# Laying the end of batch 0's latent attention beside the next stage of a hybrid two-layer kernel

## Chip, core and metric

The program runs on one core of one Trainium2 chip. The metric is the device time of one execution in microseconds (us). The time before is the median of three runs. One execution was also taken with the hardware profiler; it carries the trace that is quoted here.

## The reference, cut to what matters

Two batches of 1024 tokens with 128 channels pass through eight residual blocks. The first four are of interest:

```
x = x + latent_attention(layernorm(x))     # 16 heads, keys and values from a latent of 32, causal
x = x + spiking_ffn(layernorm(x))          # relu^2 layer, five steps of a spiking neuron: a count of spikes / 5
x = x + state_space(layernorm(x))          # convolution, per-token step sizes, a scan along the tokens
x = x + spiking_ffn(layernorm(x))
... linear attention, experts, attention over heads, experts
```

The latent attention is a softmax over earlier tokens: `softmax(mask(q k / 8)) v`, then the output projection and the residual add. Its softmax needs row maxima, exponentials, sums, the inverse of the sums and a product with it. The spiking layer reads every channel of a token after the attention has been added. The batches are independent of each other in all of these blocks.

## The kernel before

The first layer does not run block by block. While one batch is in one block, the other is in another, and the order in which the instructions stand on each engine is written out by hand: every step is a Python generator, and `weave(main, side, rate)`, `alternate(...)` and `among(...)` decide whose turn it is. Inside `tc.manual_schedule(engines=ALL)` the instructions go to the engines in just this order. Each engine works through its own queue in order, so an instruction that waits holds up all that stand behind it.

The order at the place of the change:

1. Row maxima of batch 0 (`row_maxima(0, ...)`), then its attention, `attend(0, ...)`. The attention works on two halves of 512 query tokens (`Half`), each over 4 groups of heads (`C = 4`). The end of the first half is drawn out between the steps of the second half. The end of the second half is run through alone after the last step (`for _ in end: yield`).
2. `Half.end()` is that end: ScalarE copies the sums (`rec`, L438), VectorE takes the reciprocal (L439), and then, for each of the four groups, TensorE spreads the inverse sums over the rows with a matmul by `pick` (L446) and VectorE multiplies `oU` by them (L454). Sixteen matmuls by `wvo` (L459) give the projected output in PSUM, and VectorE adds it to the tokens `x_res` (L469).
3. Constants of the state space (`StateConstants`) come next in the program.
4. The next stage is `weave(into_space(0, bank), maxima, 1.1)`. Its main stream is `into_space(0, ...)`: spiking layer of tokens 0 to 511, spiking layer of tokens 512 to 1023 beside the first tokens of the state space, then the rest of the projections and step sizes of the state space. Its side stream is `maxima = row_maxima(1, ...)`, the row maxima of batch 1: 48 units, each of four (or, where a block touches the diagonal, eight) matmuls (L265, L274) into two PSUM tiles, and two VectorE reductions (L283). After each step of the main stream `due` grows by 1.1 and as many units follow. After the 48 units the maxima are split into three bf16 terms (L288 to L297), turned by TensorE (L301) and copied to `nmT` (L302).
5. The loop of the state space of batch 0, `space[0].loop(...)`, in 32 iterations: SyncE loads two tiles of 512 KB (`s_a` and `s_h`, L751) from DRAM, ScalarE makes decays (L760), VectorE multiplies, scans and multiplies (L791, L792, L793). Woven into it as side stream is `attend(1, ...)`, the attention of batch 1, which needs `nmT` (L364).

What the loads of step 5 need: the step sizes of the first 128 channels, which VectorE finishes in `s_delta` (L713) and `s_dtx` (L715) and SyncE writes to DRAM (L714, L716); and the place of the buffers of stage 4 in SBUF, of which the last read is the matmul by `skip_wT` (L618).

PSUM has 8 banks. In step 4 two of them are the pool `bank`, which the main stream rotates through, and six are the three two-bank tiles of the maxima, `a_s`. In step 2 the tiles `a_st` of the attention are used.

The last steps of the main stream in step 4 come from `alternate(s.first_sizes(1), s.rest(1))`. On TensorE they are the products by `wb8T`, by `wc8T`, by `skip_wT`, by `wd2T` and again by `skip_wT` (all L618).

Of the kernel before, what the change touches and what calls it, by code (L numbers as in the profile page):

```python
# [9 lines left out]
F32 = mybir.dt.float32  # L10
# [9 lines left out]
P = 128  # L20
# [71 lines left out]
def weave(main, side, rate):  # L92

    due = 0.0
    for _ in main:
        due += rate
        while due >= 1.0:
            next(side, None)
            due -= 1.0


def alternate(*streams):

    streams = list(streams)
    while streams:
        for steps in list(streams):
            try:
                next(steps)
            except StopIteration:
                streams.remove(steps)  # L110
                continue
            yield
# [16 lines left out]
def drain(steps):  # L129
    for _ in steps:  # L130
        pass
# [20 lines left out]
class LatentAttention:  # L152
# [149 lines left out]
        nc.vector.tensor_copy(self.nmT[b], pt.rearrange("p a b -> p (a b)"))  # L302
        yield

    def attend(self, b, work, ps, ps_o, added=False, beside=iter(())):

        halves = [self.Half(self, b, half, work, ps, ps_o, added) for half in range(2)]  # L310
        units = [(h, c, kb) for h in halves for c in range(self.C) for kb in range(h.last + 1)]
        n = len(units)
        held, end = {}, iter(())

        for step in range(n + 3):
            if step < n:
                h, c, kb = units[step]
                held[step] = h.exponentials(c, kb)
            for back in (2, 3):
                if 0 <= step - back < n:  # L320
                    h, c, kb = units[step - back]
                    if back == 2:
                        h.weigh(c, kb, *held.pop(step - 2))
                    elif added and kb == h.last:
                        h.total_denominators(c)
                    if back == 2 + added and c == self.C - 1 and kb == h.last:
                        drain(end)
                        end = h.end()
            next(end, None)
            yield  # L330
        for _ in end:
            yield
            next(beside, None)
        yield from beside

    class Half:


        def __init__(self, latent, b, half, work, ps, ps_o, added):
            self.latent, self.b, self.half = latent, b, half  # L340
            self.work, self.ps, self.ps_o, self.added = work, ps, ps_o, added
            self.last = 4 * half + 3
            self.oTs, self.total = {}, {}

# [63 lines left out]
        def weigh(self, c, kb, pTs, off):  # L408
            latent, nc = self.latent, self.latent.g.nc
            last = kb == self.last  # L410
            if kb == 0:
                self.oTs[c] = self.ps_o.tile([P, 512], F32, name="a0_oT")
            for j in range(latent.J):
                nc.tensor.matmul(
                    self.oTs[c][32 * j : 32 * j + 32, off:],
                    latent.lat[self.b][:, kb, :],
                    pTs[j // 2][:, j % 2, off:],
                    start=(kb == 0),
                    stop=last,
                )  # L420
            if not self.added:
                self.denominators(c, pTs, off, c == 0 and kb == 0, c == latent.C - 1 and last)
            elif kb > 0:
                for k, pT in enumerate(pTs):
                    total = self.total[c, k][:, :, off:]
                    nc.vector.tensor_add(total, total, pT[:, :, off:])
            if last:
                if c == 0:
                    self.oU = self.work.tile([P, latent.C, 512], F32, name="a0_oU")
                nc.scalar.copy(self.oU[:, c, :], self.oTs.pop(c))  # L430

        def end(self):


            latent, g, nc, C = self.latent, self.latent.g, self.latent.g.nc, self.latent.C
            oU = self.oU
            rec = self.work.tile([P, 512], F32, name="a0_rec")
            nc.scalar.copy(rec, self.dT)  # L438
            nc.vector.reciprocal(rec, rec)  # L439
            yield  # L440
            if self.half == 0:
                for _ in range(2):
                    yield
            for c in range(C):
                rr = self.ps.tile([P, 2, 512], F32, name="a0_st")
                nc.tensor.matmul(rr[:, 0, :], latent.pick[:, c, :], rec, start=True, stop=True)  # L446
                if self.half == 0:
                    rs = self.work.tile([P, 512], F32, name="a0_rs", bufs=2)
                    nc.scalar.copy(rs, rr[:, 0, :])
                    nc.vector.tensor_mul(oU[:, c, :], oU[:, c, :], rs)  # L450
                    if c % 2:
                        yield
                else:
                    nc.vector.tensor_mul(oU[:, c, :], oU[:, c, :], rr[:, 0, :])  # L454
            yield
            pf = self.ps.tile([P, 2, 512], F32, name="a0_st")[:, 0, :].rearrange("p (a b) -> p a b", a=4)
            for i in range(4):
                for c in range(C):
                    nc.tensor.matmul(  # L459
                        pf[:, i, :], oU[:, c, bass.ts(i, P)], latent.wvo[:, c, :], start=(c == 0), stop=(c == C - 1)  # L460
                    )
            t = self.b * TPB + 4 * self.half
            xt = g.x[:, t : t + 4, :]
            if self.half == 0:
                add = self.work.tile([P, 4, D], F32, name="a0_rs", bufs=2)
                nc.scalar.copy(add, pf)
                nc.gpsimd.tensor_add(xt, xt, add)
            else:
                nc.vector.tensor_add(xt, xt, pf)  # L469
            yield  # L470
# [1032 lines left out]
def first_layer(g, w, open_experts, load_expert):  # L1503
# [3 lines left out]
    def pool(stack, name, bufs, **kw):  # L1507
        return stack.enter_context(tc.tile_pool(name=name, bufs=bufs, **kw))
# [5 lines left out]
    right = dict(side="right")  # L1514
    ends, latents, spaces = ExitStack(), ExitStack(), ExitStack()
    latent = LatentAttention(g, w, pool(latents, "a0_keep", 1, **right))
    own = pool(latents, "a0_batch1", 1, **right)
    with ExitStack() as es:
        latent.project([pool(es, "a0_batch0", 1), own])
        with tc.tile_pool(name="a0_seq", bufs=1) as seq, tc.tile_pool(name="a0_ps_a", bufs=2, space=PSUM) as ps:  # L1520
            drain(latent.row_maxima(0, seq, ps, 4))
        work = pool(es, "a0_work", 2)
        ps, ps_o = pool(es, "a0_ps_b", 3, space=PSUM), pool(es, "a0_ps_o", 1, space=PSUM)
        with tc.manual_schedule(engines=ALL):
            drain(latent.attend(0, work, ps, ps_o, added=True))

    bank = banks(spaces, "bank", 2)
    shared = StateConstants(g, w, pool(spaces, "s_one", 1))
# [43 lines left out]
    with tc.manual_schedule(engines=ALL):  # L1572
        with (
            tc.tile_pool(name="a0_seq", bufs=1, **right) as aseq,
            tc.tile_pool(name="a0_ps_a", bufs=3, space=PSUM, **right) as ps,
        ):
            maxima = latent.row_maxima(1, aseq, ps, 2)
            weave(into_space(0, bank), maxima, 1.1)
            drain(maxima)
        work = pool(latents, "a0_work", 1, **right)  # L1580
        ps, ps_o = pool(latents, "a0_ps_b", 2, space=PSUM, **right), pool(latents, "a0_ps_o", 1, space=PSUM, **right)

        spikes = spiking_steps(g, w, [2], Borrowed(work), lambda name: ps.tile([P, 2, 512], F32, name="a0_st")[:, 0, :])
        attend = latent.attend(1, work, ps, ps_o, beside=spikes)
        with tc.tile_pool(name="s_work", bufs=1, reuse_waits="tile") as work:
            side = among(space[0].late(), attend, 2)
            weave(space[0].loop(work, bank), side, 2.1)
        drain(side)
        latents.close()
        open_experts()  # L1590
        behind = batch0_behind()
        next(behind)
        with ExitStack() as es:
            weave(into_space(1, banks(es, "bank1", 3, **right), begun=True), behind, 0.85)
        with tc.tile_pool(name="s_work", bufs=1, reuse_waits="tile") as work:
            side = among(space[1].late(), behind, 2)
            weave(space[1].loop(work, bank), side, 2.1)
        spaces.close()
        with ends, ExitStack() as es:
            weave(out_of_space(1, banks(es, "bank", 3), abreast=True), side, 0.5)  # L1600
            drain(side)
# [115 lines left out]
```

## Time and profile before

| | us |
|---|---|
| median of three runs | 2140.3 (2138.62 to 2142.33) |
| the profiled execution, its own time | 2130.55 |
| span of the trace in it | 2128.5 |

| engine | busy us | share of the span |
|---|---|---|
| TensorE (PE) | 1844.5 | 87% |
| VectorE (DVE) | 1590.1 | 75% |
| ScalarE (ACT) | 1146.8 | 54% |
| GpSimd (POOL) | 923.6 | 43% |

Times in the profile count from the start of the span. The shares are means over the whole program; the change lies at 266 to 437 us, where the shares are others. A matmul on 32-bit operands shows as two passes, so four instructions are "x8" in a row. "PEclk" is the TensorE clock that was granted, as a share of full speed. "Idle before" is time in which the engine had nothing running ahead of the instruction, with the one that released it. "SPq" is SyncE's queue, which issues DMAs.

### The profile page before, as it was taken

What the parts mean: (1) busy time and instruction counts of PE and PEld (TensorE: products, weight loads), DVE (VectorE), ACT (ScalarE), POOL (GpSimd) and SP (SyncE); (2) the same over time, 40 slices, a digit from 0 to 9 for tenths busy, and PEclk for the clock granted to TensorE, in tenths of its full rate; (3) what the DMA queues carried; (4) which work ended last, traced back from release to release, by engine and by line L of the source; (5) the groups of instructions that cost most, each with busy time, mean ns of one, the idle gap of its engine ahead of it and who ended that gap; (6) DMA issues with size and microseconds to landing.
All of it is one profiled execution on the core that took longest, in us unless ns stands there. A gap on an engine that the chain in (4) does not pass through costs nothing. (4 is left out here: it accounts for less than half of the span.)

```text
span 2128.5 us, 29668 instructions
## 1 busy us (share of the span) xinstructions
PE 1844.5 (87%) x11616; PEld 1011.0 (47%) x11616; DVE 1590.1 (75%) x1846; ACT 1146.8 (54%) x1577; POOL 923.6 (43%) x510
## 2 busy tenths in 40 slices
PE   7679888979977757899678899999999999999999
PEld 4223243323334422334356565666565666566754
DVE  5976866898775679896432798999899999998222
ACT  1026612265643457683433677777777777777422
POOL 1013411055411210000110288989898888989400
PEclk9989978989997978999899999999999999999999
DMA  4000000097643077660000466666666666666000
GB/s 94 1 1 2 1 1 1 20 213 173 156 113 119 11 168 180 156 155 4 0 1 0 111 176 159 178 167 182 163 174 169 179 176 176 169 179 180 14 6 5
DMA packets 73771, 219.73 MB, mean 103 GB/s; under 512 B 9184, under 2 KB 19872, under 8 KB 73504
## 3 DMA queue, kind: packets, MB, share of 16 engines
q1 hardware_dynamic: 54736, 149.40, 23.8%
q0 software_dynamic: 18432, 67.12, 16.5%
q8 instruction: 91, 1.49, 0.3%
q10 hardware_dynamic: 464, 1.33, 0.3%
q14 instruction: 48, 0.39, 0.1%
HBM read 78.35 MB, written 5.24 MB: 39 GB/s over the span
## 5 line engine op out<-in xcount | busy, mean ns | idle before, releaser
L1345 POOL TENSOR_TENSOR h_e<-h_e,h_r 128x2048 f32<-128x2048 f32 x128 | 601.6, 4705 | 71.5 <-ACT h_r L1330 40.1
L1290 ACT ACTIVATE h_e<-h_e 128x1024 f32<-128x1024 f32 x256 | 256.6, 1049 | 165.5 <-DVE h_e L1287 164.8
L1281 DVE TENSOR_REDUCE h_m<-h_s 128x128 f32<-128x2048 f32 x128 | 293.2, 2290 | 52.1 <-PE h_s L1270 49.2
L1287 DVE TENSOR_TENSOR h_e<-h_s,h_m 128x2048 f32<-128x2048 f32 x128 | 293.2, 2290 | 9.1 <-DVE h_m L1281 0.5
L381 POOL TENSOR_SCALAR_AFFINE_SELECT a_pT<-a_pT 128x256 f32<-128x256 f32 x120 | 131.7, 1120 | 203.5 <-ACT a_pT L378 200.8
L283 DVE TENSOR_REDUCE a_nm<-a_s 128x2 f32<-128x1024 f32 (+7 forms) x144 | 168.1, 1217 | 40.4 <-PE a_s L274 26.2
L1270 PE MATMUL h_s<-h_qz,h_kT 32*128 32x512 f32 x1024 | 147.6, 645 | 40.2 <-DVE h_e L1287 38.8
L1111 PE MATMUL h_po<-e_h,Wd 128*128 128x256 f32 x640 | 172.2, 388 | 3.8 <-DVE e_h L1070 2.1
L378 ACT ACTIVATE a_pT<-a_st 128x1024 f32<-128x1024 f32 (+3 forms) x176 | 129.9, 791 | 64.9 <-PE a_st L364 63.4
L792 DVE TENSOR_TENSOR_SCAN s_h<-s_a,s_h 128x1024 f32<-128x1024 f32 x64 | 148.7, 2323 | 18.4 <-ACT s_a L760 14.4
L1298 POOL DMA_DIRECT2D h_e<-h_e x128 | 132.2, 1033 | 61.9 <-DMA h_e<-h_e 46.3
L1303 PE MATMUL h_pd<-ident,h_e 128*128 128x128 f32 x1024 | 138.4, 278 | 16.9 <-DMA h_e<-h_e 10.1
L1303 PEld LDWEIGHTS h_pd<-ident,h_e 128*128 128x128 f32 x1024 | 113.4, 141 | 79.7 <-DMA h_e<-h_e 34.2
L265 PE MATMUL a_s<-a_latT,a_qT 32*128 32x512 f32 (+3 forms) x768 | 115.8, 584 | 40.4 <-DVE a_nm L283 38.3
L1350 PE MATMUL h_po<-h_e,h_vz 128*32 128x256 f32 x2048 | 138.4, 388 | 0.8 <-POOL h_e L1345 0.6
L355 PE MATMUL a_st<-a_qT,a_latT 32*128 32x512 f32 (+3 forms) x768 | 119.2, 554 | 9.2 <-ACT a_pT L378 7.0
L958 ACT ACTIVATE e_sg<-e_pg 128x512 f32<-128x512 f32 x96 | 57.3, 597 | 129.5 <-PE e_pg L955 107.0
L1111 PEld LDWEIGHTS h_po<-e_h,Wd 128*128 128x128 f32 x640 | 111.9, 192 | 30.9 <-DVE e_h L1070 16.1
L963 DVE TENSOR_TENSOR e_h<-e_sg,e_pu 128x512 f32<-128x512 f32 x96 | 64.5, 684 | 82.3 <-PE e_pu L956 70.2
L956 PE MATMUL e_pu<-e_uT,Wu 128*128 128x512 f32 x192 | 102.0, 613 | 19.7 <-DVE e_h L963 19.7
L1084 PE MATMUL e_pgu<-e_uT,Wg 128*128 128x256 f32 x480 | 115.9, 382 | 0.0
L1084 PE MATMUL e_pgu<-e_uT,Wu 128*128 128x256 f32 x480 | 115.0, 380 | 0.5 <-ACT e_sg L1090 0.5
(303 smaller groups left out, 3203.9 us busy)
## 6 DMA issues: line engine op xcount, KB each, us to landing
h_e<-h_e SPq DMA_DIRECT2D x128, 512.0 KB, 3.4
h_e<-h_e POOLq DMA_DIRECT2D x128, 512.0 KB, 5.0
s_a<-s_steps SPq DMA_DIRECT2D x64, 512.0 KB, 5.1
s_h<-s_steps SPq DMA_DIRECT2D x64, 512.0 KB, 6.6
s_steps<-s_gate SPq DMA_DIRECT2D x8, 256.0 KB, 2.0
Wg<-in_Wg_dram SPq DMA_DIRECT2D x8, 256.0 KB, 5.9
Wu<-in_Wu_dram SPq DMA_DIRECT2D x8, 256.0 KB, 5.9
Wd<-in_Wd_dram SPq DMA_DIRECT2D x8, 256.0 KB, 6.0
```

What stands on the lines that cost most here:

```text
L283: nc.vector.tensor_reduce(nm[:, half, i, h : h + together], s[:, :, :n], AX.X, ALU.max, negate=True)
L792: nc.vector.tensor_tensor_scan(h, a, h, 0.0, ALU.mult, ALU.add)
L1084: self.g.nc.tensor.matmul(pgu[:, k, :], self.w[name][:, e, bass.ts(fc, P)], uT, start=True, stop=True)
L1111: nc.tensor.matmul(self.sums, self.w["Wd"][:, e, fc, :], h, start=False, stop=last, skip_group_check=True)
L1270: nc.tensor.matmul(s[:, j, :].rearrange("p (k q) -> p k q", k=K), kTs[b][quad, bass.ts(kb, P)], qzs[b][qb // 4][quad, :, bass.ts(qb % 4, P ...
L1281: nc.vector.tensor_reduce(m, heads.rearrange("p h q -> p q h"), AX.X, ALU.max)
L1287: nc.vector.tensor_sub(e, heads, m.unsqueeze(1).to_broadcast([P, H, P]))
L1290: nc.scalar.activation(eh, eh, AF.Exp, scale=scale)
L1298: nc.gpsimd.dma_start(out=e2, in_=e[:, 8:16, :], accum_op=ALU.add)
L1303: nc.tensor.matmul(pd[:, t, :], pair[:, t, k, :], g.ident, start=(t == 0 and k == 0), stop=(k == 7), is_transpose=True, skip_group_check=True,
L1345: nc.gpsimd.tensor_mul(e, e, r.unsqueeze(1).to_broadcast([P, H, P]))
L1350: nc.tensor.matmul(po[32 * j : 32 * j + 32, :], vz[:, kb * J + j, two].rearrange("p a d -> p (a d)"), a[:, 4 * j + 2 * two : 4 * j + 2 * t ...
```

## The change

`attend` takes a pool `late`. With it, the tiles `oU` and `rec` of the second half lie in that pool, which stays open through the next stage, and `attend` hands back the rest of the end instead of running through it. The copy of the sums and the reciprocal are still issued in `attend`. The rest of the end, from the first `pick` matmul on, becomes a stream of six steps: one for each group, one bare step, and one with the sixteen `wvo` matmuls and the add. This stream alternates with the steps of `into_space(0, ...)` in the main stream of step 4. Its PSUM tiles come from the two-bank pool `bank`.

```diff
-    def attend(self, b, work, ps, ps_o, added=False, beside=iter(())):
+    def attend(self, b, work, ps, ps_o, added=False, beside=iter(()), late=None):
         halves = [self.Half(self, b, half, work, ps, ps_o, added) for half in range(2)]
+        halves[1].keep = late or work
...
             next(end, None)
             yield
+        if late:
+            self.left_over = halves[1], end
+            return
         for _ in end:
...
+            self.bank = lambda: ps.tile([P, 2, 512], F32, name="a0_st")[:, 0, :]
...
-            rec = self.work.tile([P, 512], F32, name="a0_rec")
+            rec = self.keep.tile([P, 512], F32, name="a0_rec")
...
             for c in range(C):
-                rr = self.ps.tile([P, 2, 512], F32, name="a0_st")
-                nc.tensor.matmul(rr[:, 0, :], latent.pick[:, c, :], rec, start=True, stop=True)
+                rr = self.bank()
+                nc.tensor.matmul(rr, latent.pick[:, c, :], rec, start=True, stop=True)
...
                 else:
-                    nc.vector.tensor_mul(oU[:, c, :], oU[:, c, :], rr[:, 0, :])
+                    nc.vector.tensor_mul(oU[:, c, :], oU[:, c, :], rr)
+                    if self.keep is not self.work:
+                        yield
             yield
-            pf = self.ps.tile([P, 2, 512], F32, name="a0_st")[:, 0, :].rearrange("p (a b) -> p a b", a=4)
+            pf = self.bank().rearrange("p (a b) -> p a b", a=4)
...
+    late = ExitStack()
+    late_pool = pool(late, "a0_late", 1, **right)
...
-            drain(latent.attend(0, work, ps, ps_o, added=True))
+            drain(latent.attend(0, work, ps, ps_o, added=True, late=late_pool))
...
-            weave(into_space(0, bank), maxima, 1.1)
+            half, end = latent.left_over
+            half.bank = lambda: bank("a0_end")
+            weave(alternate(end, into_space(0, bank)), maxima, 1.1)
             drain(maxima)
+        late.close()
```

The instructions are the same in kind and number, save for their places in the queues of TensorE and VectorE; the queues of ScalarE, GpSimd and SyncE keep their order.

More of the change, by code (lines that the diff above doesn't have):

```diff
@@ L340, in __init__ @@
             self.latent, self.b, self.half = latent, b, half
-            self.work, self.ps, self.ps_o, self.added = work, ps, ps_o, added
+            self.work, self.ps, self.ps_o, self.added, self.keep = work, ps, ps_o, added, work
+            self.bank = lambda: ps.tile([P, 2, 512], F32, name="a0_st")[:, 0, :]
             self.last = 4 * half + 3
@@ L428, in weigh @@
                 if c == 0:
-                    self.oU = self.work.tile([P, latent.C, 512], F32, name="a0_oU")
+                    self.oU = self.keep.tile([P, latent.C, 512], F32, name="a0_oU")
                 nc.scalar.copy(self.oU[:, c, :], self.oTs.pop(c))
@@ L444, in end @@
             for c in range(C):
-                rr = self.ps.tile([P, 2, 512], F32, name="a0_st")
-                nc.tensor.matmul(rr[:, 0, :], latent.pick[:, c, :], rec, start=True, stop=True)
+                rr = self.bank()
+                nc.tensor.matmul(rr, latent.pick[:, c, :], rec, start=True, stop=True)
                 if self.half == 0:
                     rs = self.work.tile([P, 512], F32, name="a0_rs", bufs=2)
-                    nc.scalar.copy(rs, rr[:, 0, :])
+                    nc.scalar.copy(rs, rr)
                     nc.vector.tensor_mul(oU[:, c, :], oU[:, c, :], rs)
```

## Prediction

> **What bounds the kernel now.** I first read the end of the attention in the timeline, since that stretch is what is moved. Columns: start, busy time, engine, line, operation, tiles; in brackets, idle time and releaser.
>
> ```profile
> 262.49 3.34 DVE L439 RECIPROCAL a_rec<-a_rec 128x512 f32<-128x512 f32 x1
> ...
> 265.97 6.15 PE L446 MATMUL a_st<-a_rec,a_pick 128*128 128x512 f32 x8 [4.93 <-DVE a_rec L439]
> ...
> 271.96 4.11 PE L459 MATMUL a_st<-a_wvo,a_oU 128*128 128x128 f32 x32
> ...
> 276.11 0.69 DVE L469 TENSOR_TENSOR x_res<-x_res,a_st 128x512 f32<-128x512 f32 x1 [3.26 <-PE a_st L459]
> ...
> 276.95 0.50 PE L265 MATMUL a_s<-a_latT,a_qT 32*128 32x128 f32 x8 [0.87 <-DVE x_res L469]
> ```
>
> From 265.97 to 276.95 nothing runs but this chain; VectorE is busy 3.4 of these 11 us and the maxima of batch 1 need none of it. That is what can be won. The windows then show the stage that is to take the work: first the end itself, then the stage up to and from the point where the second `s_ln` is done (L711), then the loop.
>
> ```profile
> core 0: us, PE busy (x) PEld busy (x) DVE busy (x) ACT busy (x) POOL busy (x), PEclk, DMA share, GB/s
> 276.70:414.40 137.70, 121.87 (x614) 53.80 (x614) 98.66 (x162) 26.99 (x37) 16.51 (x21) 0.84 0.01 4
> 414.40:437.30 22.90, 17.29 (x75) 5.85 (x74) 20.47 (x25) 5.49 (x6) 0.00 (x0) 0.95 0.38 95
> ...
> 437.30:500.00 62.70, 53.02 (x476) 18.21 (x476) 60.98 (x45) 43.44 (x58) 44.35 (x31) 0.86 0.97 227
> 500.00:600.00 100.00, 97.97 (x876) 34.61 (x872) 78.21 (x52) 65.28 (x79) 37.51 (x27) 1.00 0.64 153
> ```
>
> The receiving stage is not free: TensorE is busy 121.87 of 137.70 us, with 15.8 idle, VectorE 98.66. After it the loop is bound by VectorE (60.98 of 62.70) and then by TensorE (97.97 of 100), so when the loop starts decides everything later. Last, the timeline of the seam, VectorE, TensorE, SyncE and ScalarE:
>
> ```profile
> 413.75 0.69 DVE L711 TENSOR_TENSOR s_ln<-s_ln,s_dtx 128x512 f32<-128x512 f32 x1
> 414.36 4.61 DVE L283 TENSOR_REDUCE a_nm<-a_s 128x2 f32<-128x1024 f32 x4
> ...
> 422.26 0.69 DVE L715 TENSOR_TENSOR s_dtx<-s_delta,s_xc 128x512 f32<-128x512 f32 x1
> ...
> 433.49 0.22 DVE L288 TENSOR_TENSOR a_nm<-a_nm 128x64 f32<-128x64 f32 x1
> ...
> 436.74 0.69 DVE L302 COPY a_nmT<-a_mt 128x1024 bf16<-128x1024 bf16 x1 [1.20 <-PE a_mt L301]
> 437.35 1.22 DVE L791 TENSOR_TENSOR s_h<-s_h,s_Bx 128x1024 f32<-128x1024 f32 x1
> ...
> 427.86 1.13 PE L618 MATMUL s_pm<-s_xnT,skip_wT 128*128 128x512 f32 x2
> ...
> 429.02 0.61 SPq L751 DMA_DIRECT2D s_a<-s_steps  x1
> ...
> 433.86 1.15 ACT L760 ACTIVATE s_a<-s_a,s_negA 128x1024 f32<-128x1024 f32 x1 [2.94 <-DMA s_a<-s_steps]
> ...
> 438.41 1.15 ACT L760 ACTIVATE s_a<-s_a,s_negA 128x1024 f32<-128x1024 f32 x1 [3.40 <-DMA s_a<-s_steps]
> ```
>
> The last `skip_wT` product frees the buffers, SyncE issues the loads at 429.02, the first `s_a` lands 4.8 us later and the first `s_h` at 436.1 (the issue view gives its shortest landing, 6.3 us from 429.79). Meanwhile VectorE works through the last maxima and L288 to L302, to 437.4. So the loop's first loads are covered by maxima.
>
> **What moves.** ScalarE, GpSimd and SyncE keep their order. On TensorE and VectorE two things happen. First, the end is cut into single instructions between units of maxima. Second, the main stream has six more steps, and at 1.1 units a step six to seven units are drawn ahead of where they stood. In the order of before, seven units (14 reductions) and then L288 to L302 stand behind L711; in the changed order no unit does, and L288 to L302 come directly behind L711, ahead of L713, L715 and, on TensorE, ahead of four of the last L618 products.
>
> **The start: 9.2 us won.** The reciprocal is not moved and the first `pick` matmul still stands ahead of the first unit on TensorE, so the wait of 4.93 us at 261 to 266 stays. Behind that one matmul (two passes at 0.85 us, as the 6.15 us row spaces eight) the first unit can start at 267.7 instead of 276.95: 9.2 us earlier.
>
> **The work up to L711: 16.7 us of TensorE or 19.9 us of VectorE more.** The end brings 9.99 us of TensorE (its window 265.80:276.70) less the 1.7 of the first matmul: 8.3. The seven units bring, at 1.07 us for four matmuls of 512 columns (337.38 to 338.45) and 0.23 for the four mask matmuls of every other one, 8.4. On VectorE the end brings five instructions of 0.69, 3.4, and the units 7 x 2.35 = 16.5. If the idle time of the pacing engine stays as it is, L711 shifts by -9.2 + 16.7 = +7.5 where TensorE paces and by -9.2 + 19.9 = +10.7 where VectorE does. Both pace in turn: a unit's third tile waits for a reduction ("DVE a_nm L283" ends 33.1 us of the weight loads' waits, "PE a_s L274" 23.6 us of VectorE's). I take the middle, +9.1. Bounds: +10.7 above. Below, all 15.8 us of TensorE's idle time could be filled, giving -8.3, but a part stands where VectorE runs the spike counts (waits of 3.60 and 4.56 us before L265 at 301.98 and 357.39), which stay in one piece; I bound it at half filled, 7.5 - 7.9 = -0.4. L711 then ends at 414.44 + 9.1 = 423.5.
>
> New waits inside: each `pick` product must be read by VectorE before its bank comes round again. Behind it on TensorE stand units, the transposes and the L549 matmuls of the spikes, and ScalarE's relus wait for those. VectorE has two to four reductions ahead of a multiply at that place (up to 2.6 us for 256 columns), and ten ahead of L469, of 256 and 384 columns (2 x 1.29 + 3 x 1.81 = 8.0 us). I cost these at nothing extra, since TensorE has units to run until its tiles are full; without that cover it is up to 8.0 us once, at the fourth L549. The tokens that L469 delivers late are read by the second spiking layer only after the first one's counts, so that is covered.
>
> **The seam: 3.9 us won for the loads.** From L711's end: L288 to the end of the turning matmuls is 436.71 - 433.49 = 3.2 us (435.70 plus 1.01). Then TensorE has four products left, by `wc8T` 1.87, `skip_wT` 1.05, `wd2T` 1.05, `skip_wT` 1.06, spaced as at 412.80, 421.61, 425.53 and 427.86: 5.0 us at the full clock, 10.1 at half. ScalarE must clear the banks between (0.58, a table load of 1.28, 0.60), which fits in. The wait of 4.52 us for the terms, ahead of the turning at 435.70, now stands before these products, and after the other wait of that length, where no matmul starts from 298.4 to 302.0, the windows show a granted clock of 0.54 for 300 to 320. So I take 7.5, midway. The loads go out 3.2 + 7.5 = 10.7 us behind L711 instead of 429.02 - 414.44 = 14.6, so 3.9 less (1.3 to 6.4). L713, L715 and the two writes (landing 2.0 us) end near 7.6 us behind L711, earlier, so they do not decide.
>
> The Trainium skill (TensorE: Matmul & The Clock Gate, "What's actually happening") says that an idle window of about 3.4 us halves the clock until a busy one has passed. The trace's 0.54 after that wait agrees; by the rule alone the products would take the full 10.1 us and the sum would be 2.6 us higher.
>
> **The sum.** Loads: +9.1 - 3.9 = +5.2, issued at 434.2. First L791: the `s_h` load lands 7.1 us after the first issue, 441.3 against 437.35, so +4.0; VectorE has nothing to run in front of it any more. The attention's first exponentials stand behind the second L760 on ScalarE, which waits for the second `s_a`: +5.2. TensorE fills 500 to 600 with that attention, so I carry +5.2. In the profiled execution: 2130.55 + 5.2 = 2135.8. That execution is 9.75 us under the median; carried to the median, 2140.3 + 5.2 = **2145.5 us**, slower.
>
> **Rivals.** *The idle time takes the work* (other side: faster). Place: the waits of TensorE between 276.7 and 414.4, 15.8 us. If more than 9 us of them go to moved work, L711 shifts by less than -0.4 and the loads by less than -4.3; all of it would give -12.2, 2128. It decides from a shift of L711 under +3.9, where the loads break even. For it: both engines have idle time at once. Against: the two engines wait for each other through three tiles, and more units between the same space steps lengthen those waits. Chance 0.09. *Won at the front, given back at the seam, near even*: 3.5 to 9 us of idle filled, L711 between -0.4 and +8, 2136 to 2144.6. Chance 0.28. *One more stretch at half clock*: 300 to 320 ran at 0.54 with 15.78 us busy, so another such stretch costs some 8 us: 2153.5. For it: TensorE now waits at other places, with the clock at 0.84 in this stage already. Chance 0.10. *The change hides nothing* can be left out as a case: the order shows the units between the `pick` matmuls. My own forecast holds 0.53.
>
> **How the numbers follow.** About 0.2%, 4.3 us, is what a measurement of this kernel can tell from no change. Slower: 0.53 + 0.10 = 0.63. Same: 0.28. Faster: 0.09. The range reaches down into the near-even case, to 2138, and up over VectorE pacing and the half clock (+10.7 - 1.3 = +9.4, 2149.7) into the clock rival, to 2152.5.
>
> **What the next profile would show.** Right: the first L265 of the stage near 267.7; the copy to `nmT` ahead of `s_delta`; four L618 products at a lower clock behind the turning; the loads near 434; VectorE idle for some 8 us before the first L791, where it now goes without a pause. Wrong: L711 ending before 418, loads issued before 429, or a first L791 before 437; then the rival of the filled idle time holds. If the loop starts late but the program does not end late, TensorE's stretch from 500 to 600 had slack that I deny.

## The result, and the profile after

| | before | after |
|---|---|---|
| median of eleven runs each, us | 2139.13 (2134.11 to 2145.97) | 2149.38 (2143.14 to 2154.65) |
| profiled execution, own time, us | 2130.55 | 2149.37 |
| its span, us | 2128.5 | 2147.4 |

The changed kernel takes 1.0043 times as long, 95% interval 1.0029 to 1.0056. It is slower: the ratio, taken of 2139.13, makes it about 9.2 us (6.2 to 12.0); the two medians lie 10.25 apart.

The two profiled executions may not be compared by the time of day. The reciprocal of the sums stands ahead of everything that is changed, yet it starts at 262.49 in the one and at 269.64 in the other; over all the traces of this study it lies between 262.5 and 270.1. Below, times are therefore counted from the start of the reciprocal. In the kernel after, lines of the attention's end are 5 higher and lines of the state space 7 higher than before (L446 is L451, L711 is L718, L751 is L758, L791 is L798).

The timeline of the kernel after, where the end used to run alone:

```profile
269.64 3.34 DVE L444 RECIPROCAL a_rec<-a_rec 128x512 f32<-128x512 f32 x1
...
273.03 2.08 PE L451 MATMUL a_end<-a_rec,a_pick 128*128 128x512 f32 x2 [4.84 <-DVE a_rec L444]
...
275.04 0.81 PE L265 MATMUL a_s<-a_latT,a_qT 32*128 32x128 f32 x8
275.14 0.69 DVE L459 TENSOR_TENSOR a_oU<-a_oU,a_end 128x512 f32<-128x512 f32 x1 [2.17 <-PE a_end L451]
```

The first unit of maxima starts 5.40 us behind the reciprocal's start instead of 14.46: 9.06 us earlier. The wait for the reciprocal is where it was.

The windows of the kernel after: the start, the stage up to the second `s_ln`, the seam, and the loop.

```profile
core 0: us, PE busy (x) PEld busy (x) DVE busy (x) ACT busy (x) POOL busy (x), PEclk, DMA share, GB/s
269.60:275.00 5.40, 1.97 (x2) 0.50 (x2) 3.37 (x3) 0.00 (x0) 0.00 (x0) 0.77 0.01 3
275.00:433.30 158.30, 134.97 (x709) 62.00 (x708) 117.89 (x180) 26.98 (x37) 16.51 (x21) 0.83 0.01 4
433.30:452.20 18.90, 8.81 (x30) 3.50 (x30) 5.69 (x12) 5.49 (x6) 0.00 (x0) 0.77 0.47 122
...
500.00:600.00 100.00, 97.79 (x902) 35.21 (x904) 82.79 (x56) 64.73 (x82) 47.09 (x35) 1.00 0.66 161
```

The row to compare with the second one, a window of the kernel before from its first unit to the end of the second `s_ln`:

```profile
276.90:414.40 137.50, 121.87 (x614) 53.80 (x614) 98.46 (x160) 26.99 (x37) 16.51 (x21) 0.84 0.01 4
```

Idle time is the length less the busy time. The stage is 20.80 us longer. VectorE's busy time grew by 19.43 and its idle time by 1.37 (39.04 to 40.41). TensorE's busy time grew by 13.10 and its idle time by 7.70 (15.63 to 23.33). So the change as a whole did not fill TensorE's idle time; it made more of it.

The timeline at the seam after:

```profile
432.63 0.69 DVE L718 TENSOR_TENSOR s_ln<-s_ln,s_dtx 128x512 f32<-128x512 f32 x1
433.24 0.22 DVE L288 TENSOR_TENSOR a_nm<-a_nm 128x64 f32<-128x64 f32 x1
...
435.42 1.01 PE L301 MATMUL a_mt<-a_identb,a_terms 128*128 128x128 bf16 x8 [6.37 <-DVE a_terms L294]
...
436.23 3.68 PE L625 MATMUL s_pm<-s_xc,wc8T 128*128 128x512 f32 x4
436.47 0.69 DVE L302 COPY a_nmT<-a_mt 128x1024 bf16<-128x1024 bf16 x1 [1.20 <-PE a_mt L301]
...
442.49 1.13 PE L625 MATMUL s_pm<-s_xnT,skip_wT 128*128 128x512 f32 x2 [0.67 <-ACT s_gate L700]
443.65 0.61 SPq L758 DMA_DIRECT2D s_a<-s_steps  x1
...
448.21 1.15 ACT L767 ACTIVATE s_a<-s_a,s_negA 128x1024 f32<-128x1024 f32 x1 [2.66 <-DMA s_a<-s_steps]
...
450.88 1.23 DVE L798 TENSOR_TENSOR s_h<-s_h,s_Bx 128x1024 f32<-128x1024 f32 x1 [8.27 <-DMA s_h<-s_steps]
```

No reduction stands behind the second `s_ln` any more. The turning of the maxima follows at once, TensorE waits 6.37 us for it, and the product by `wc8T` behind that wait takes 3.68 us. In the kernel before it takes 1.94:

```profile
412.80 1.94 PE L618 MATMUL s_pm<-s_xc,wc8T 128*128 128x512 f32 x4
```

The loads go out 10.3 us behind the end of the second `s_ln`. VectorE then idles 8.27 us, with nothing left that could cover the first loads.

### The profile page after: what moved, and what is told of

Read it like the earlier page. It is cut to its first block, busy times and chain, and to the rows that moved or that the text cites. A ratio compares the mean times of both kernels' runs of the same rounds, so it can differ in the third digit from the quotient of the medians.

```text
span 2147.4 us, 29665 instructions
## 1 busy us (share of the span) xinstructions
PE 1854.3 (86%) x11616; PEld 1018.1 (47%) x11616; DVE 1589.5 (74%) x1846; ACT 1146.5 (53%) x1577; POOL 916.7 (43%) x510
## 5 line engine op out<-in xcount | busy, mean ns | idle before, releaser
L386 POOL TENSOR_SCALAR_AFFINE_SELECT a_pT<-a_pT 128x256 f32<-128x256 f32 x120 | 125.0, 1061 | 207.7 <-ACT a_pT L383 204.6
L283 DVE TENSOR_REDUCE a_nm<-a_s 128x2 f32<-128x1024 f32 (+7 forms) x144 | 168.4, 1216 | 43.8 <-PE a_s L274 22.0
L1118 PEld LDWEIGHTS h_po<-e_h,Wd 128*128 128x128 f32 x640 | 112.3, 193 | 31.1 <-DVE e_h L1077 16.1
```

Source lines behind the costliest of these rows:

```text
L283: nc.vector.tensor_reduce(nm[:, half, i, h : h + together], s[:, :, :n], AX.X, ALU.max, negate=True)
L1118: nc.tensor.matmul(self.sums, self.w["Wd"][:, e, fc, :], h, start=False, stop=last, skip_group_check=True)
```

## The experiments

**Theory 1, drawing ahead:** the six added steps in the main stream draw seven units of maxima in front of the second `s_ln`. These cost more there than they save behind it, and behind the loads' issue nothing is left to cover them. Laying the end beside other work is a gain by itself. **Theory 2, cutting up:** the end's chain, cut into single instructions between units, with the waits between TensorE and VectorE that it brings, costs the time.

All kernels in one table. Milestones are us from the start of the reciprocal in the profiled execution, in brackets the difference from before. "Behind" counts the reductions of the maxima (L283, two to a unit) that the trace shows behind the second `s_ln`; kernels with the same count stand alike at the seam. The ratio is to runs of the kernel before on the same chip. The milestones are of one execution each: fill1 and fill1_again are the same kernel, and theirs differ by 2.1 us, so less than that tells nothing.

| kernel | behind | end of second `s_ln` | first load issued | first scan | ratio of times (95%) |
|---|---|---|---|---|---|
| before | 14 | 151.95 | 166.53 | 176.18 | 1 |
| after | 0 | 163.69 (+11.7) | 174.01 (+7.5) | 182.57 (+6.4) | 1.0043 (1.0029 to 1.0056) |
| steps_only | 0 | 168.78 (+16.8) | 179.16 (+12.6) | 187.74 (+11.6) | 1.0048 (1.0030 to 1.0067) |
| spread | 12 | 145.96 (-6.0) | 158.28 (-8.3) | 167.93 (-8.3) | 0.9962 (0.9945 to 0.9979) |
| hold3 | 6 | 160.74 (+8.8) | 163.70 (-2.8) | 179.59 (+3.4) | 1.0013 (0.9993 to 1.0032) |
| half_reduce | 0 | 159.84 (+7.9) | 169.86 (+3.3) | 179.32 (+3.1) | 1.0026 (1.0014 to 1.0038) |
| before106 | 16 | 149.77 (-2.2) | 163.67 (-2.9) | 177.46 (+1.3) | 1.0001 (0.9989 to 1.0014) |
| rate094 | 14 | 141.97 (-10.0) | 153.68 (-12.9) | 165.39 (-10.8) | 0.9960 (0.9944 to 0.9975) |
| rate090 | 18 | 141.12 (-10.8) | 152.30 (-14.2) | 168.93 (-7.3) | 0.9959 (0.9944 to 0.9974) |
| rate092 | 16 | 143.33 (-8.6) | 155.65 (-10.9) | 170.24 (-6.0) | 0.9978 (0.9961 to 0.9994) |
| fill1 | 14 | 141.38 (-10.6) | 153.08 (-13.4) | 164.80 (-11.4) | 0.9931 (0.9913 to 0.9949) |
| fill1_again | 14 | 139.25 (-12.7) | 150.96 (-15.6) | 162.67 (-13.5) | 0.9934 (0.9911 to 0.9956) |
| fill2 | 14 | 143.41 (-8.5) | 155.12 (-11.4) | 166.84 (-9.3) | 0.9965 (0.9949 to 0.9981) |

**steps_only: the drawing ahead without the end.** On the kernel before, six empty steps alternate with the main stream; the end stays where it was.

```diff
-            weave(into_space(0, bank), maxima, 1.1)
+            weave(alternate(iter(range(6)), into_space(0, bank)), maxima, 1.1)
```

> The kernel before, with six empty steps alternating with the first steps of the main stream: nothing of the end is moved, but the weave draws the maxima of batch 1 six to seven units ahead, as in the change. Theory 1 (the drawing ahead is what costs): no 9.1 us at the start; seven units of 512 columns, 8.4 us on TensorE to 16.5 on VectorE, come ahead of the last s_ln (L711), and the loads then go out about 4 us closer behind it. Loads 8 to 13 us later than before, first L791 7 to 12 us later, the program 7 to 12 us slower (0.3 to 0.6%). Theory 2 (the cutting up of the end costs: waits between TensorE and VectorE, clock): within 2 us of the kernel before.

Measured: 1.0048, not to be told from the whole change, with the end of the second `s_ln` 16.8 us later. The timeline of this kernel, its reciprocal and its seam:

```profile
265.55 3.34 DVE L439 RECIPROCAL a_rec<-a_rec 128x512 f32<-128x512 f32 x1
...
433.64 0.69 DVE L711 TENSOR_TENSOR s_ln<-s_ln,s_dtx 128x512 f32<-128x512 f32 x1
434.25 0.22 DVE L288 TENSOR_TENSOR a_nm<-a_nm 128x64 f32<-128x64 f32 x1
...
444.71 0.61 SPq L751 DMA_DIRECT2D s_a<-s_steps  x1
...
451.96 1.23 DVE L791 TENSOR_TENSOR s_h<-s_h,s_Bx 128x1024 f32<-128x1024 f32 x1 [8.19 <-DMA s_h<-s_steps]
```

It has the same bare seam, 8.19 us of idle VectorE included, without any of the end in it. Its window from the first unit to the end of the second `s_ln`:

```profile
279.90:434.30 154.40, 129.95 (x670) 58.19 (x670) 114.60 (x175) 26.98 (x37) 16.50 (x21) 0.84 0.01 4
```

Against the row of before, the stretch is 16.90 us longer, VectorE's busy time 16.14 and its idle time 0.76 (39.04 to 39.80); TensorE's busy time grew by 8.08 and its idle time by 8.82. Seven units cost VectorE's price for them, and hardly anything else. TensorE's added idle time is here without the end, so it comes with the units and not with the moved work.

**spread: the end beside other work, with hardly any drawing ahead.** On the kernel after, 48.4 units (44 steps at 1.1) are spread over 50 steps: a rate of 0.97. One unit is still ahead of its place in the kernel before (12 reductions behind instead of 14).

```diff
-            weave(alternate(end, into_space(0, bank)), maxima, 1.1)
+            weave(alternate(end, into_space(0, bank)), maxima, 0.97)
```

> The changed kernel with one number changed, the rate of the weave 0.97 instead of 1.1, so that 48 units fall on 50 main steps as evenly as they fell on 44 before. The end is still cut up and laid beside the stage. Theory 1: the seam is as before (maxima and the copy to nmT behind the last s_ln, covering the loads), the start keeps its 9.1 us, and the end's 8.3 us of TensorE or 3.4 us of VectorE come back: the loop starts 1 to 6 us earlier than in the kernel before, and the program is 1 to 6 us faster than it, some 10 us faster than the changed kernel. Theory 2: the loop starts 4 or more us later than before, as in the changed kernel.

Measured: 0.9962, faster than before, by about 8 us where 1 to 6 were expected; the loop starts 8.3 us earlier, where 1 to 6 were expected too. The end is cut up exactly as in the change, so theory 2 falls as the cause of the loss. The timeline of this kernel:

```profile
269.78 3.34 DVE L444 RECIPROCAL a_rec<-a_rec 128x512 f32<-128x512 f32 x1
...
415.05 0.69 DVE L718 TENSOR_TENSOR s_ln<-s_ln,s_dtx 128x512 f32<-128x512 f32 x1
...
428.06 0.61 SPq L758 DMA_DIRECT2D s_a<-s_steps  x1
...
432.54 0.22 DVE L288 TENSOR_TENSOR a_nm<-a_nm 128x64 f32<-128x64 f32 x1
...
435.78 0.69 DVE L302 COPY a_nmT<-a_mt 128x1024 bf16<-128x1024 bf16 x1 [1.19 <-PE a_mt L301]
436.39 1.22 DVE L798 TENSOR_TENSOR s_h<-s_h,s_Bx 128x1024 f32<-128x1024 f32 x1
```

The maxima lie over the loads again, and the first multiply by `s_Bx` follows the copy without a pause. Its window from the first unit to the end of the second `s_ln`:

```profile
275.10:415.70 140.60, 124.78 (x661) 56.35 (x660) 103.83 (x168) 26.99 (x37) 16.50 (x21) 0.86 0.01 4
```

Against the row of before, TensorE's idle time is what stayed here (15.63 to 15.82), and VectorE's fell (39.04 to 36.77).

The two parts of the change do not simply add up. Kernels with the same count behind the second `s_ln` can be compared in pairs, without and with the end laid beside. It brings the second `s_ln` 10.0 us nearer from before to rate094 and 6.4 us from before106 to rate092, but only 5.1 us from steps_only to after. In time the first pair shows 0.40%, the second 0.23% with intervals that overlap a little, the third (1.0048 and 1.0043) nothing that can be told from noise. Seen the other way, drawing seven units ahead costs 16.8 us without the end laid beside (before to steps_only) and 21.7 us with it (rate094 to after). So the loss is of the drawing ahead, and beside it the end laid beside wins less. A part of these differences can be the 2.1 us of scatter; why the two work against each other was not followed.

**hold3: the change with its last three units held back.** They then stand behind the whole main stream, over the loads.

```diff
-            weave(alternate(end, into_space(0, bank)), maxima, 1.1)
+            weave(alternate(end, into_space(0, bank)), islice(maxima, 45), 1.1)
             drain(maxima)
```

> The changed kernel at its rate of 1.1, but the weave draws only 45 of the 48 units; the last three, with the copy to nmT, follow the last step of the main stream. Theory 1: three units (7 us of VectorE) and the 3.9 us of L288 to L302 leave the path ahead of the loads, which go out about 8 to 10 us earlier than in the changed kernel, and VectorE runs the three units while they land; the loop then starts when nmT is copied, 3 to 7 us earlier than in the changed kernel, so the program lands within 4 us of the kernel before. Theory 2: no difference from the changed kernel (10 us slower than before).

Measured: loads 10.3 us earlier than in the kernel after, the first scan only 3.0. The timeline of this kernel:

```profile
427.62 0.69 DVE L718 TENSOR_TENSOR s_ln<-s_ln,s_dtx 128x512 f32<-128x512 f32 x1 [0.79 <-ACT s_ln L715]
...
431.28 0.61 SPq L758 DMA_DIRECT2D s_a<-s_steps  x1
...
442.00 0.23 DVE L288 TENSOR_TENSOR a_nm<-a_nm 128x64 f32<-128x64 f32 x1
...
445.24 0.69 DVE L302 COPY a_nmT<-a_mt 128x1024 bf16<-128x1024 bf16 x1 [1.20 <-PE a_mt L301]
445.85 1.22 DVE L798 TENSOR_TENSOR s_h<-s_h,s_Bx 128x1024 f32<-128x1024 f32 x1
```

The bound has changed sides: the data are there (the first multiply no longer waits for a load), and VectorE reaches it only when it is through with the maxima. It is not busy all that time: from the end of the second `s_ln` to the first scan it works 12.7 of 18.9 us, at a granted TensorE clock of 0.57, and it waits 3.20 and 1.35 us for the matmuls of the three units. Both must be met, the loads early and the maxima finished when they land.

**half_reduce: does VectorE pace the stage?** In the kernel after, the last block's reductions of a pair read half of their columns.

```diff
-s[:, :, :n]
+s[:, :, : n // 2 if together == 2 and i == TPB - 1 else n]
```

> The changed kernel, but for the last block of 128 queries of batch 1 VectorE takes its maxima over half of the columns; all matmuls stay. This leaves out part of the maxima. It asks which engine paces the units that are drawn ahead: each reduction of 2 x 512 columns falls from 1.22 us to 0.68, 14 of them ahead of the last s_ln, 7.5 us less on VectorE and nothing less on TensorE. If VectorE paces: the last s_ln 6 to 8 us nearer to the reciprocal than in the changed kernel (156 to 158 us instead of 163.7), loads and loop as much earlier, the program about 7 us faster than the changed kernel. If TensorE paces: within 2 us of the changed kernel.

Measured: neither. The end of the second `s_ln` comes 3.9 us earlier than in the kernel after, and the time is 1.0026. The window of this kernel that answers to the stage above:

```profile
267.90:422.30 154.40, 132.95 (x709) 61.10 (x708) 109.95 (x180) 26.99 (x37) 16.50 (x21) 0.84 0.01 4
```

VectorE has 7.9 us less to do than after, and 4.0 of them turn into idle time (40.41 to 44.45). What is taken off VectorE is won only by half, as if TensorE, some 4 us behind it, came to pace the stage; that is a reading, not shown. How the pace passes from the one to the other inside the stage was not followed.

**before106: is it the lower rate alone?** The kernel before, with the rate 1.06 in place of 1.1.

> The kernel before, with the rate of the weave 1.06 instead of 1.1: the end of batch 0 runs alone as before, and two units fewer are drawn ahead of the last s_ln. It asks whether the gain of the runs at 0.97 and 0.94 is one of the rate alone. If so, this is faster than before by 5 us or more. If the gain is the 9.1 us at the start, the loads go out 2 to 4 us earlier but the loop still waits for the copy to nmT, which comes after the same units: within 3 us of the kernel before.

Measured: 1.0001. Fewer units before the second `s_ln` help the loads by 2.9 us, but the loop then waits for the maxima, and the first scan is 1.3 us later. Both differences in the milestones are near what one execution can tell. A lower rate alone wins nothing; the gain of spread comes from the end laid beside other work.

**rate094 and rate090: still fewer units in front of the seam.** As spread, with 0.94 and 0.90.

> As the run with rate 0.97, at 0.94: one or two more units stay behind the last s_ln. Theory 1: the loads go out one to three us earlier still and the loop start is set by the copy to nmT; the program 2 to 8 us faster than the kernel before, the same as or up to 3 us faster than at 0.97. Theory 2: 4 or more us slower than before.

> As the runs at 0.97 and 0.94, at 0.90: three or four more units stay behind the last s_ln than at 0.97. The loads go out earlier than at 0.94, but the copy to nmT starts the loop, after the same sum of units: the loop start within 3 us of that at 0.94 (165.4 us after the reciprocal), the program 5 to 11 us faster than the kernel before.

Measured: 0.9960 and 0.9959, not to be told from spread. Rate094 has the count of the kernel before behind the second `s_ln`, so it is the plain test of laying the end beside: 0.40% faster. From 0.94 to 0.90 the loads gain 1.4 us and the first scan loses 3.5, where 3 at most were expected: the maxima are the later of the two again. Over these rates the program's time is flat, also where the first scan is 3.5 us later.

**fill1: a unit for the wait that nobody filled.** TensorE waits 4.84 us ahead of the first `pick` matmul in the kernel after, and the change leaves that wait alone. One unit of maxima is put in front of that matmul; the rate is 0.92. Two kernels serve as controls: rate092 has the same rate without that unit, and so one unit more behind the second `s_ln`; rate094 has the same number of units behind it.

```diff
-            weave(alternate(end, into_space(0, bank)), maxima, 1.1)
+            next(maxima)
+            weave(alternate(end, into_space(0, bank)), maxima, 0.92)
```

> The changed kernel at a rate of 0.92, with one unit of maxima ahead of the first pick matmul, so that TensorE has it to run while VectorE takes the reciprocal (4.9 us of waiting before). The unit, 1.0 us at the full clock and 1.4 at half, and its place later go: loop start 0 to 3 us earlier than at 0.94, the program 7 to 12 us faster than the kernel before.

> The changed kernel at a rate of 0.92, no unit ahead of the first pick matmul: the control of the run with one unit ahead, which was 0.7% faster than the kernel before. If that gain was of the rate, this is within 0.15% of it. If the unit in the wait for the reciprocal makes a part, this is 2 to 5 us slower than with it, 0.4 to 0.5% faster than before.

> The same kernel as the run with one unit ahead, once more beside its control on one chip: 0.5 to 0.8% faster than the kernel before.

Measured: 0.9931, and in the second run 0.9934, more than the 7 to 12 us expected. Rate092 has 0.9978, some 10 us more where 2 to 5 were expected; the intervals do not overlap (0.9956 at most against 0.9961 at least). Against rate094, which stands alike at the seam, and rate090 the difference is smaller, 0.0025 to 0.0029, and the ends of the intervals touch (0.9949 and 0.9956 against 0.9944). The timelines of the second fill1 kernel and then of rate092:

```profile
263.10 0.50 PE L265 MATMUL a_s<-a_latT,a_qT 32*128 32x128 f32 x8 [0.69 <-ACT a_rec L443]
263.54 0.40 PE L274 MATMUL a_s<-a_mask,a_identb 128*128 128x128 bf16 x4
...
263.87 3.34 DVE L444 RECIPROCAL a_rec<-a_rec 128x512 f32<-128x512 f32 x1
...
267.26 2.07 PE L451 MATMUL a_end<-a_rec,a_pick 128*128 128x512 f32 x2 [3.33 <-DVE a_rec L444]
```

```profile
270.10 3.34 DVE L444 RECIPROCAL a_rec<-a_rec 128x512 f32<-128x512 f32 x1
...
273.50 1.65 PE L451 MATMUL a_end<-a_rec,a_pick 128*128 128x512 f32 x2 [4.84 <-DVE a_rec L444]
```

The unit's matmuls run from 263.10 to 263.94, just ahead of the reciprocal, and shorten TensorE's wait from 4.84 to 3.33 us. The first `pick` matmul starts no earlier for it: 3.39 us behind the reciprocal's start with the unit, 3.40 without. So what the unit wins directly is its own 0.8 us of TensorE, while the medians lie some 10 us apart from rate092 (2124.0 and 2124.8 against 2134.8) and some 5 to 6 from rate094 (2129.8). The first scan is 5.4 and 7.6 us earlier than in rate092, but only 0.6 and 2.7 us earlier than in rate094. The windows from the reciprocal to the first scan, of the second fill1 kernel, of rate092 and of rate094:

```profile
263.90:426.50 162.60, 137.59 (x725) 61.05 (x728) 126.42 (x192) 33.52 (x44) 16.50 (x21) 0.90 0.09 22
```

```profile
270.10:440.30 170.20, 145.70 (x736) 63.09 (x740) 126.30 (x193) 33.52 (x44) 16.50 (x21) 0.86 0.10 25
```

```profile
264.95:430.34 165.39, 140.74 (x736) 61.25 (x740) 126.45 (x193) 33.63 (x44) 16.40 (x21) 0.87 0.08 22
```

VectorE does the same work in all three. TensorE is busy 8.1 us less than in rate092, at a granted clock of 0.90 instead of 0.86, and 3.1 us less than in rate094, at 0.90 instead of 0.87; 0.8 us of either is the unit, which runs ahead of the window. That the unit changes the clock is argued, not shown, and two figures speak against a direct effect. In the first 42 us around the reciprocal the clock is not higher with the unit (0.92) than in rate092 (0.96). And the first fill1 run, the same kernel, shows 0.88 and 139.8 us of TensorE, close to rate094's 0.87 and 140.7. That fill1 is faster is measured; why it is faster by more than its unit stays open.

**fill2: two units in the wait.** Two units ahead of the first `pick` matmul, at a rate of 0.90.

> Two units ahead of the first pick matmul, at a rate of 0.90. The three two-bank tiles hold one and a half units, so the second unit's second half waits for a reduction that stands behind the reciprocal, and the first pick matmul behind it comes about 1 us later than with one unit; the wait of TensorE is filled with half a unit more. Within 2 us of the run with one unit ahead.

Measured: 0.9965, 7 us slower than fill1, where a difference of 2 at most was expected. Two units are not better than one. The trace shows a part: the second unit's second half waits 3.19 us for a reduction that stands behind the reciprocal, and the first `pick` matmul starts 4.79 us behind the reciprocal's start instead of 3.39. That is 1.4 us; the rest stays open. **fill1 is the best version found**, faster than the kernel before and the changed one by 0.66 to 0.69% and by 1.1% (0.9931 / 1.0043 = 0.989).

## Why the prediction was right, and by which step too low

The forecast of a slower kernel held, 2145.5 against 2149.38, inside the range and above its middle. By its own steps:

- *The start.* Said 9.2 us earlier, with the wait for the reciprocal kept: 9.06, wait 4.84.
- *The work up to the second `s_ln`.* Said +9.1, the middle of +7.5 and +10.7; measured +11.7. This is the step that was mis-sized. The middle stood for both engines pacing in turn. For this change the windows show VectorE's account alone: its idle time stayed near where it was, 39.04 before, 39.80 in steps_only and 40.41 after, and its busy time carried the shift: for seven units 16.5 were said and 16.14 measured, for the end 3.4 were said and 19.43 - 16.14 = 3.3 measured. TensorE's price for the units was right as well, 8.4 said and 8.08 measured, but for the end it was too high, 8.3 said and 13.10 - 8.08 = 5.0 measured, and its idle time, which the step let stay or be filled, grew by 8.82 in steps_only. So the upper end, +10.7, came closest, as seen afterwards; the windows of before alone do not say which account holds, and in spread it is TensorE's idle time that stayed. It is short by 1.0, which is 0.1 for the start and 1.4 for VectorE's idle time, less 0.5 that the work was priced too high. Half_reduce limits the reading: with 7.9 us less on VectorE its idle time does grow, by 4.0.
- *The seam.* Said: loads 10.7 us behind the second `s_ln` instead of 14.6, with four products at a lowered clock. Measured 10.3, with a granted clock of 0.77 in the window of the seam and 3.68 us for the `wc8T` product instead of 1.94. From the end of the turning, 435.42 + 1.01, to the end of the last `skip_wT`, 442.49 + 1.13, it is 7.2 us, where 7.5 was taken, midway between full and half clock. From the page "TensorE: Matmul & The Clock Gate" of the Trainium skill ("What's actually happening") the prediction had worked out 10.1 us, with all four products at half clock. That is not what the page says: by its table a busy window of about 3.4 us brings the full clock back. The seam agrees with that: the granted clock is 0.53 from 436.2 to 440.0, where the first product runs, and 1.00 from 440.0 to 443.7. The stretch that the prediction named in support does not: in the kernel before TensorE is busy without a break from 302 to 310, and the clock stays at 0.50.
- *The loads and the loop.* Said +5.2 and +4.0; measured +7.5 and +6.4. Both are high by 2.3 and 2.4, which is the 2.6 of the step above less 0.4 at the seam. The first `s_h` landed 7.2 us behind the first issue (7.1 said), and VectorE idled 8.27 us in front of it (some 8 said).
- *Carried to the end.* Said +5.2. In the profiled executions the scans run +5.8 to +7.6 late to the end of batch 1's loop, and the end of the span +11.8. The ratio makes the program's shift about 9.2 (6.2 to 12.0), so most of it is as large as the loop's late start, 6.4 to 7.5. The rest is open: from the first scan to the end the executions of all kernels take 1688 to 1698 us, with no order by when the loop starts (steps_only, the latest, 1688.4; fill1_again, the earliest, 1693.0; rate092, between them, 1698.4).
- *The waits at the banks.* Costed at nothing. The first spike counts run 11.1 us late, the second only 6.5, so a part was given back, and at the seam one wait of 0.67 us is seen. VectorE waited 4.1 us in all for `pick` products and 1.9 for the `wvo` products, where 8.0 were named as the most without cover. Its idle time in the stage grew by only 1.37, so little of these waits shows in the shift.
- *The rivals.* Idle time takes the work: refuted, with a shift of +11.7 where it needed one under +3.9, and with TensorE's idle time up by 7.7 us. Near even: refuted by the interval, 1.0029 at least, and by the same shift, which it put at +8 at most. (The idle times that these two rivals name do not give the shifts beside them: 7.5 - 9 is -1.5 and not -0.4, and 7.5 - 3.5 is +4 and not +8. It decides nothing, since no idle time was filled.) One more stretch at half clock: not seen as such, 0.83 after against 0.84 before in the stage.

The conclusion that the prediction did not draw: both halves of its sum were in its own numbers, 9.2 us won at the start less 3.4 for the end, and 16.5 lost by drawing ahead. The second is not a property of the end laid beside other work, but of a rate that was left at 1.1 while the main stream grew by six steps. With the rate set for 50 steps, the same change is a gain of 0.38%. Its numbers could not show that the two do not add up: at the second `s_ln` the end laid beside won 5.1 us with the units drawn ahead and 10.0 without.

## What to carry to other kernels

When steps are added to a stream that draws a second stream at a fixed rate, recount where the last unit of the second stream falls: here it moved in front of the seam and left the first loads uncovered. Where two engines both have idle time, do not average their two prices: a window before and after tells which of them kept its idle time. It need not always be the same one. With seven units drawn ahead, which cost VectorE 16.1 us and TensorE 8.1, VectorE kept it; with the end laid beside (spread), TensorE did. Where two things meet at a loop's start, here the loads and the maxima, the later one is the wait, so moving one of them alone soon wins nothing: from a rate of 0.97 to 0.90 the time was flat. And choose the control that stands alike at the place that decides: fill1 looks nearly twice as good beside the kernel of its own rate as beside the one with the same units behind the seam.

## What the runs showed of the hardware

The work from the reciprocal to the first scan is the same in rate090, fill1, fill1_again, fill2, rate094, spread, rate092 and hold3 (VectorE is busy for 126 to 127 us in each), but the stretch lasts 162.6 us at a granted TensorE clock of 0.90 (fill1_again), 164.8 at 0.88 (fill1), 165.4 at 0.87 (rate094), 170.2 at 0.86 (rate092) and 179.6 at 0.80 (hold3); fill2 with 166.8 at 0.85, spread with 167.9 at 0.86 and rate090 with 168.9 at 0.84 lie off that line. So a longer stretch goes along with a lower clock, and the differences are larger than the work that was moved. But the clock is not the whole of it: TensorE is busy 148.6 us in hold3 and 148.3 in rate090, so that the 10.7 us by which hold3 is longer are idle time of TensorE. A part is scatter, too: fill1 and fill1_again are the same kernel. Whether the order sets the clock or both follow from the waits was not settled.

A long wait is not needed for half clock. In hold3 the longest idle time of TensorE between 405 and 431 is 1.43 us, and from 432 to 440 the granted clock is 0.50, with TensorE busy for 7.8 of these 8 us.
